# Turning the second image's columns back on ScalarE with accumulating transfers, residuals in the banks, and seven products one group earlier

## The chip, the cores and the metric

One core of a Trainium2 chip. The metric is the device time of one execution in microseconds (us), the median of several executions. The core's engines run side by side, each with a queue of its own: TensorE (PE in the profile) multiplies matrices out of SBUF, the on-chip memory of 128 partitions, into PSUM banks; VectorE (DVE) and ScalarE (ACT) work on SBUF and PSUM; GpSimd (POOL) does elementwise work and issues some transfers; SyncE (SP) only issues transfers. An instruction starts when the one ahead of it in its queue is done and what it waits for has come, so one late operand holds up everything behind it on that engine.

## The reference

The input is two images of 56 x 56 positions (tokens) with 384 channels in float32, 6272 tokens in all, and two layers. Cut to what matters here (LN is a layer norm over channels, gelu the exact one):

```
# layer 0: neighbourhood attention (7 x 7, 12 heads), then a two-layer product
x = x + attention(LN(x)) @ w_proj + b_proj
x = x + gelu(LN(x) @ w1 + b1) @ w2 + b2            # 384 -> 1536 -> 384
# layer 1: convolution and four directional scans, then a two-layer product
p     = LN(x) @ w_in + b_in                        # 384 -> 768
local = depthwise_conv_3x3(p)
mixed = 0.25 * (lr(local) + rl(local) + tb(local) + bt(local)) + local
x = x + LN(mixed) @ w_out + b_out                  # 768 -> 384
x = x + gelu(LN(x) @ w1' + b1') @ w2' + b2'
```

`lr`, `rl`, `tb` and `bt` are running averages y[i] = 0.6 y[i-1] + 0.4 x[i] along the rows, forwards and backwards, and along the columns, both ways. `mixed` of one image needs the whole image: the last row of a column scan depends on the first.

## The kernel before, in words

**Phases.** The attention comes first and takes the first 815 us or so; the change doesn't touch it. Then `passes` runs two passes over groups of four tiles of 128 tokens (512 tokens). The first pass (`groups`, one single tile and twelve fours) does the two-layer product of layer 0 for group g and, one group behind, the projection by w_in (`project_in`), which stores p by channels in DRAM (`p_d`). The second pass (`dgroups`, twelve fours and a single tile) does layer 1's part behind the scans: hidden products (12 x 3 matmuls of 128x512 by `hidden`, with a GELU on ScalarE for each of the 12), the projection by w_out of the next group (`project_out`, six matmuls for each tile), and the second product (`tokens`, 12 matmuls of 128x384 for each tile, 48 for a group). I call these three stages of a group its hidden stage, its projection and its second product.

**Seven products.** From group `switch` (4) on, the second pass does a group's two products in another form: matrices are split in two by two blocks, and seven block products with sums around them take the place of eight (`hidden_by_seven`, `tokens_by_seven`). It needs sums of the weights' blocks (`sums_of_w1`, five subtractions, and `sums_of_w2`, four), sums of the group's input (`sums_of_input`, four, whose tile is `xsums`), all on GpSimd, and room in SBUF that the convolution's buffers (the pool `conv`) hold until it has ended.

**The convolution beside.** The convolution and the scans are jobs that an object `Beside` deals out in steps between the products. `beside.go(worth, own)` adds to an allowance of VectorE time (times `rate`, less the stage's own VectorE work) and takes steps while there is allowance left; a step is what lies between two `yield`s, and the number yielded is its estimated cost. `beside.later(issue, n)` puts an instruction off by n steps, so that an engine's queue gets it when what it waits for is near. `beside.behind()` looks at the next job, starts its loads and returns it. `beside.until(name)` runs all that is left up to a job, at once.

A `Band` (a block of 128 channels, up to 28 rows of an image) loads p, multiplies the centre tap (ScalarE, `centre`, L1283), adds eight taps on VectorE (L1301), stores the result to `loc_d` and `mix_d` (SyncE, L1309), scans it along the rows in both directions (VectorE, `both_ways`), scales it (ScalarE, L1316), and adds it into `mix_d` by an accumulating transfer that GpSimd issues (`add_to_mix`, L1320). There is a `Columns` for each image and channel block, once the image's bands are done: it loads `loc_d` (two halves, L1337), turns rows into columns (`turn`: for each half of the columns four copies of 128x392, L1344, by GpSimd for the first half of a job that nothing turned ahead, else by ScalarE), and scans the two sets of columns in both directions in place; then it turns the result back while it adds it to `mix_d`: `mixed` is loaded from `mix_d`, VectorE adds the scaled lines to it (`scalar_tensor_tensor`, L1369, four for each channel block), and `mixed` is stored to `mix_d`.

**Order.** Within an engine the order is the order of the calls in the code; no scheduler moves instructions. So the steps of the convolution fall between the products where the allowance runs out. In the first pass `beside.go` is called after each product; image 1's bands come up from group to group, its columns must be done before the last group of the pass, and image 2's bands and columns run on into the second pass, up to the switch.

**The second pass's plain groups.** For each tile `tokens` fills a PSUM bank (two banks, in turns), VectorE adds the residual to it (`tensor_tensor`, L1922) and SyncE stores the tile to the output (L1923). In the last plain group, ahead of the first tile, `beside.until((1, NI - 1))` finishes the convolution, `cctx.close()` gives its room back, and the sums of weights are issued. The first pass has a different form here: there the residual is copied into the bank ahead (`seeded`, by ScalarE), the products are added to it, and ScalarE copies the sum out (L1855). The layer norm of mixed goes through the row sums that `measure` takes of the transposed input (L1405) and a factor that `project_out` applies (L1446).

Of the kernel before, what the change touches and what calls it, by code (L numbers as in the profile page):

```python
# [33 lines left out]
F32 = mybir.dt.float32  # L34
# [79 lines left out]
class Beside:  # L114
# [29 lines left out]
    def run(self):  # L144
        while True:
            self.idle = not self.jobs
            if self.idle:
                yield None
                continue
            if not self.jobs[0].loaded:  # L150
                self.jobs[0].load()
                yield 5.0
            job = self.jobs.pop(0)
            yield from job.steps()
            self.finished.add(job.name)
# [21 lines left out]
def block_kernel(ctx: ExitStack, tc: tile.TileContext, ins: dict, out: bass.AP):  # L177
# [914 lines left out]
    def passes(xs, xn, w1, w2, between=lambda ps: None):  # L1092
# [9 lines left out]
        switch = 4  # L1102
# [132 lines left out]
        def flat(t):  # L1235
            return t.rearrange("p a b -> p (a b)")
# [20 lines left out]
        class Band:  # L1257
# [21 lines left out]
            def centre(self):  # L1279
                if self.loc is None:  # L1280
                    self.loc = half("loc", "work", 3)
                    r = self.lo - self.top
                    nc.scalar.activation(  # L1283
                        flat(self.loc[:, : self.n]), flat(self.pt[:, r : r + self.n]), AF.Copy,
                        scale=self.tap(0, 0),
                    )

            def steps(self):
                beside.behind(Band)
                if self.loc is None:  # L1290
                    self.centre()
                    yield 2.5
# [15 lines left out]
                for to in (loc_d, mix_d):  # L1308
                    beside.later(lambda to=to: nc.sync.dma_start(  # L1309
                        out=to[self.b][self.m, :, at], in_=flat(loc)))  # L1310
                both = half("both", "out", 4)[:, : self.n]
                yield from both_ways(both, loc)
                behind = beside.behind()
                if isinstance(behind, Band):
                    behind.centre()
                beside.later(lambda: nc.scalar.mul(flat(both), flat(both), share), 8)  # L1316
# [5 lines left out]
        class Columns:  # L1322
# [27 lines left out]
            def steps(self):  # L1350
                if not self.lines:

                    self.turn(nc.gpsimd.tensor_copy)
                    yield 2.5
                mixed, behind = [], None
                for c in range(2):
                    t = self.lines[c]
                    for step, took in enumerate(both_ways(t, t)):
                        if c == 0 and step == 0:
                            self.turn(nc.scalar.copy)  # L1360
                            for h in range(2):
                                mixed.append(half("mixed", "out", 4))
                                nc.sync.dma_start(out=flat(mixed[h]), in_=self.rows(mix_d, h))
                        yield took
                    if c == 1:
                        behind = beside.behind()
                    for h in range(2):
                        to = mixed[h][:, :, c * HALF : (c + 1) * HALF]
                        nc.vector.scalar_tensor_tensor(  # L1369
                            to, t[:, :, h * HALF : (h + 1) * HALF].rearrange("p w h -> p h w"),  # L1370
                            share, to, ALU.mult, ALU.add,
                        )
                        yield us(HALF / 2, 2.0)
                    if c == 0:
                        beside.behind()
                if isinstance(behind, Columns):
                    behind.turn(nc.scalar.copy)
                for h in range(2):
                    beside.later(lambda h=h: nc.sync.dma_start(
                        out=self.rows(mix_d, h), in_=flat(mixed[h])))  # L1380
# [90 lines left out]
        def project_in(g, hT, between=lambda: None, at=1):  # L1471
# [15 lines left out]
            while bands and bands[0][0] * T1 + min(bands[0][2] + 1, H) * W <= t0 + groups[g][1] * P:  # L1487
                b, lo, hi = bands.pop(0)
                beside.jobs += [Band(b, m, lo, hi) for m in range(NI)]
                if hi == H:  # L1490
                    beside.jobs += [Columns(b, m) for m in range(NI)]
# [404 lines left out]
        beside.rate = 0.93  # L1896
        for g, (t0, n) in enumerate(dgroups[:switch]):
# [7 lines left out]
            if g == switch - 1:  # L1905

                beside.until((1, NI - 1))
                cctx.close()
                tp = pctx.enter_context(tc.tile_pool(name="tail", bufs=1, reuse_waits="tile"))
                three = wp.tile([P, NC, INNER], F32, name="w1_t", tag="w_in")  # L1910
                w1_sums = sums_of_w1(w1, three)
                w2_sums, steps = sums_of_w2(w2)
                for step in steps:
                    step()
            for k in range(n):
                if k == n - 1:
                    hT = channels(xn, dgroups[g + 1][1], *n2)
                ps = tokens(hid, w2, k)
                o = res[:, k, :]
                if k == 0:  # L1920
                    norm.shift(dgroups[g + 1][1])
                nc.vector.tensor_tensor(o, ps, o, ALU.add)  # L1922
                nc.sync.dma_start(out=yout[t0 + k * P : t0 + (k + 1) * P, :], in_=o)  # L1923
# [3 lines left out]
                beside.go(ROW, STATS)  # L1927
# [144 lines left out]
```

## Time and profile before

| | us |
|---|---|
| time, median of 3 | 2593.29 (2593.11 to 2597.07) |
| profiled execution, its own time | 2597.85 |
| span of the profiled execution | 2596.0 |
| its mean TensorE clock, of full speed | 0.994 |

Busy time of each engine by stretch, from windows on the profile (us):

| stretch | what runs | PE | DVE | ACT | POOL |
|---|---|---|---|---|---|
| 0 to 820 | attention | 804.7 | 590.1 | 438.0 | 183.3 |
| 820 to 1070 | first pass, ahead of the convolution | 248.6 | 182.4 | 102.6 | 33.1 |
| 1070 to 1540 | first pass with the convolution | 468.4 | 383.2 | 215.0 | 64.5 |
| 1540 to 2010 | rest of the first pass, plain groups of the second | 453.2 | 383.1 | 147.7 | 85.5 |
| 2010 to 2596 | groups by seven products | 581.9 | 422.4 | 173.6 | 198.9 |

How such a profile is read: a row of the timeline is a run of like instructions with its start, the time it took, the engine, the line of the code, the operation and its operands (out<-in). What stands in brackets behind it is how long the engine had been idle ahead of the row, and which instruction's end released it. An engine that is busy nearly all the time sets the span; idle time of the others matters only where the busy one waits for it.

### The profile page before, as it was taken

Reading aid. Unit: us, or ns where it says so; the run is one execution under the profiler, and the core shown is the slowest. Engines: PE = TensorE matmul, PEld = TensorE weight load, DVE = VectorE, ACT = ScalarE, POOL = GpSimd, SP = SyncE. Lnnn points to the kernel's source line nnn. Section 1 sums busy time; section 2 is a strip of 40 time slices with the busy share of each in tenths; the row PEclk is TensorE's granted clock in tenths of the full one; section 3 lists DMA queues with packets and bytes.
Section 4 is the critical chain, followed back from the end, with each engine's and each line's share of the span. In section 5 each row is a group of like instructions: output and inputs, shape, how many; then the busy total and the mean of one; then the engine's idle time right before and its main releaser. Section 6 shows DMA issues by size and latency. Waiting matters only on the chain. (4 is left out here: it accounts for less than half of the span.)

```text
span 2596.0 us, 41217 instructions
## 1 busy us (share of the span) xinstructions
PE 2556.8 (98%) x16342; PEld 1679.8 (65%) x16342; DVE 1961.2 (76%) x3660; ACT 1076.8 (41%) x1943; POOL 565.4 (22%) x593
## 2 busy tenths in 40 slices
PE   9999999999999999999999999999998999999999
PEld 5666666666788644555545555455554888888888
DVE  4888878887344389967799979878886778878871
ACT  5655555654443344433555333322332232333222
POOL 0111212121532011110211101111105233333332
PEclk9999999999999999999999999999999999999999
DMA  7423454225412356545665567855763233333210
GB/s 230 153 83 99 157 194 144 81 94 194 129 43 61 92 160 166 157 128 151 209 236 213 172 165 214 247 132 173 246 216 105 55 73 74 73 74 74 46 28 21
DMA packets 163931, 348.10 MB, mean 134 GB/s; under 512 B 12326, under 2 KB 114192, under 8 KB 161424
## 3 DMA queue, kind: packets, MB, share of 16 engines
q1 hardware_dynamic: 131568, 270.45, 30.1%
q0 software_dynamic: 27216, 48.17, 11.7%
q10 hardware_dynamic: 4944, 26.74, 3.0%
q8 instruction: 130, 2.13, 0.3%
q14 instruction: 73, 0.60, 0.1%
HBM read 181.55 MB, written 134.88 MB: 122 GB/s over the span
## 5 line engine op out<-in xcount | busy, mean ns | idle before, releaser
L1301 DVE SCALAR_TENSOR_TENSOR loc<-pt,taps,loc 128x495 f32<-128x495 f32 (+13 forms) x432 | 398.2, 922 | 118.5 <-ACT loc L1283 105.0
L1195 PE MATMUL mm<-hT,w 128*128 128x512 f32 x936 | 413.1, 596 | 6.1 <-ACT hT L272 5.3
L1195 PEld LDWEIGHTS mm<-hT,w 128*128 128x128 f32 x936 | 175.8, 191 | 216.2 <-issue 201.5
L571 ACT ACTIVATE pts<-pts 119x448 f32<-119x448 f32 (+5 forms) x396 | 210.8, 573 | 110.3 <-DVE pts L561 105.8
L561 DVE TENSOR_TENSOR pts<-sc,bias 119x448 f32<-119x448 f32 (+5 forms) x396 | 219.2, 616 | 45.9 <-PE sc L550 45.6
L1213 PE MATMUL y<-w,hid 128*128 128x384 f32 x696 | 231.4, 490 | 10.8 <-DVE xc L1922 10.8
L1213 PE MATMUL y_end<-w,hid 128*128 128x384 f32 x696 | 229.2, 486 | 0.0
L404 PE MATMUL ps<-hT,wqkv 128*128 128x448 f32 x504 | 204.8, 550 | 2.1 <-ACT vs L449 1.5
L1206 ACT ACTIVATE hid<-mm,chan 128x512 f32<-128x512 f32 x156 | 106.8, 687 | 232.3 <-PE mm L1195 232.3
L1213 PEld LDWEIGHTS y<-w,hid 128*128 128x128 f32 x696 | 132.4, 191 | 102.2 <-DVE xc L1922 11.4
L1213 PEld LDWEIGHTS y_end<-w,hid 128*128 128x128 f32 x696 | 131.8, 190 | 90.6
L1178 DVE STREAM_TRANSPOSE hT<-xn 32x96 f32<-32x96 f32 x592 | 159.6, 270 | 23.2 <-ACT xn L255 15.5
L1417 DVE STREAM_TRANSPOSE turned<-mx 32x192 f32<-32x192 f32 x464 | 171.2, 369 | 6.1
L1195 PE MATMUL mm<-hT,w_in 128*128 128x512 f32 x396 | 172.2, 593 | 1.3 <-ACT mx L1476 0.8
L404 PEld LDWEIGHTS ps<-hT,wqkv 128*128 128x128 f32 x504 | 91.3, 189 | 84.4 <-issue 74.2
L227 POOL TENSOR_TENSOR rs<-rs,mhalf 128x4 f32<-128x4 f32 (+4 forms) x55 | 60.0, 1091 | 372.1 <-DVE rs L224 362.3
L1195 PEld LDWEIGHTS mm<-hT,w_in 128*128 128x128 f32 x396 | 75.0, 190 | 96.0 <-issue 90.4
L1320 POOL DMA_DIRECT2D mix_d<-both x54 | 50.9, 942 | 365.5 <-ACT both L1316 324.3
L550 PEld LDWEIGHTS sc<-qT,kT 32*100 32x100 f32 (+3 forms) x3168 | 87.8, 169 | 46.6 <-DVE sum L580 7.6
L590 PE MATMUL o<-pts,vt 100*32 100x112 f32 (+3 forms) x3168 | 116.5, 264 | 0.5 <-ACT pts L571 0.5
L620 PE MATMUL ps<-wproj,og 128*128 128x384 f32 x294 | 107.1, 504 | 2.8 <-DVE og L533 2.1
L550 PE MATMUL sc<-qT,kT 32*100 32x112 f32 (+3 forms) x3168 | 106.5, 268 | 3.2 <-DVE pts L561 3.2
(187 smaller groups left out, 4514.0 us busy)
## 6 DMA issues: line engine op xcount, KB each, us to landing
loc<-loc_d SPq DMA_DIRECT2D x24, 784.0 KB
mixed<-mix_d SPq DMA_DIRECT2D x24, 784.0 KB
mix_d<-mixed SPq DMA_DIRECT2D x24, 784.0 KB
xa<-x_d SPq DMA_DIRECT2D x24, 768.0 KB
xa<-rows POOLq DMA_DIRECT2D x24, 768.0 KB, 7.8
bias<-in_bias_t ACTq DMA_DIRECT2D x13, 1344.0 KB
p_d<-mx SPq DMA_DIRECT2D x11, 1536.0 KB
mx<-mix_d SPq DMA_DIRECT2D x11, 1536.0 KB
```

Of the source, the lines that this page charges most:

```text
L404: nc.tensor.matmul(ps, lhsT=wqkv[:, c, m * P : (m + 1) * P], rhs=hT[:, c, half_of(n)], start=c == 0, stop=c == NC - 1,)
L550: nc.tensor.matmul(sc[i // 2][: w.keys, i % 2, q : q + TT], lhsT=kT[d, hg, w.keys_at + r * w.kc : w.keys_at + (r + w.rows) * w.kc], rhs=qT ...
L561: nc.vector.tensor_tensor(self.pts[:n, h : h + 2, lo:hi, :], sc[half][:n, :, at * TT : (at + hi - lo) * TT].rearrange("p h (c q) -> p h c ...
L571: nc.scalar.activation(t, t, AF.Exp)
L590: nc.tensor.matmul(o[i * HD : (i + 1) * HD, self.slot, :TT], lhsT=w.vt[:n, c, h * HD : (h + 1) * HD], rhs=self.pts[:n, i, c, :], start=c = ...
L620: nc.tensor.matmul(ps, lhsT=ogs[t // 7][:, c, at : at + P], rhs=wproj[:, c, :], start=c == 0, stop=c == NC - 1,)
L1178: nc.vector.transpose(hT[j : j + HD, :, k * P + i : k * P + i + HD], xn[i : i + HD, k, :].rearrange("p (c q) -> p c q", c=NC)[:, :, j : j ...
L1195: nc.tensor.matmul(ps[:, : n * P], lhsT=w[:, c, m * P : (m + 1) * P], rhs=hT[:, c, : n * P], start=c == 0, stop=c == NC - 1,)
L1206: nc.scalar.activation(t[:, : n * P], ps[:, : n * P], AF.Gelu, bias=col(b1, m))
L1213: nc.tensor.matmul(ps, lhsT=t[:, k * P : (k + 1) * P], rhs=w[:, m, :], start=m == 0 and onto is None, stop=m == len(lhs) - 1, skip_group_c ...
L1301: nc.vector.scalar_tensor_tensor(to, pt[:, lo + dy - self.top : hi + dy - self.top, xt : xt + n], self.tap(dy, dx), to, ALU.mult, ALU.add,)
L1417: nc.vector.transpose(t[j : j + HD].rearrange("p (m c) -> p m c", m=NI)[:, :, i : i + HD], mx[i : i + HD, :, k * P + j : k * P + j + HD],)
```

## The change

- `switch` is 3 instead of 4: one more group goes by seven products.
- Image 2's `Columns` no longer load `mix_d`. Their lines are scaled and turned back by ScalarE into `mixed` (`turn_back`: eight `mul` of 128x392 for each channel block), and two accumulating transfers on GpSimd's queue add it to `mix_d`. Image 1's keep the addition on VectorE.
- A plain group of the second pass copies the residual into the bank ahead (`seeded`), and ScalarE copies the sum out, in place of VectorE's addition. The end of the convolution and the sums of weights move from ahead of the group's first tile to ahead of its third (k == 2).
- Smaller moves: stores of a band come four steps later, a column's store three; the next job is looked at before a band's scans rather than behind them, and after the first scan of a set of columns; a band can have its next job's columns turned by ScalarE and a column its next job's centre tap made; a centre tap that nothing made ahead goes to VectorE; the yield behind a job's first load is 8.0 instead of 5.0; two columns that aren't loaded yet move behind newly listed bands; the second pass's rate of 0.93 is gone, and its second product no longer takes 0.75 us off each allowance.

```diff
@@ Beside.run
-                yield 5.0
+                yield 8.0
@@ passes
-        switch = 4
+        switch = 3
@@ Band
-            def centre(self):
+            def centre(self, engine=nc.scalar):
                 if self.loc is None:
...
-                    nc.scalar.activation(
-                        flat(self.loc[:, : self.n]), flat(self.pt[:, r : r + self.n]), AF.Copy,
-                        scale=self.tap(0, 0),
-                    )
+                    to, src = flat(self.loc[:, : self.n]), flat(self.pt[:, r : r + self.n])
+                    if engine is nc.scalar:
+                        nc.scalar.activation(to, src, AF.Copy, scale=self.tap(0, 0))
+                    else:
+                        nc.vector.tensor_scalar_mul(to, src, self.tap(0, 0))
 
             def steps(self):
                 beside.behind(Band)
                 if self.loc is None:
-                    self.centre()
-                    yield 2.5
+                    self.centre(nc.vector)
+                    yield us(self.n)
...
                 for to in (loc_d, mix_d):
                     beside.later(lambda to=to: nc.sync.dma_start(
-                        out=to[self.b][self.m, :, at], in_=flat(loc)))
+                        out=to[self.b][self.m, :, at], in_=flat(loc)), 4)
                 both = half("both", "out", 4)[:, : self.n]
+                behind = beside.behind()
                 yield from both_ways(both, loc)
-                behind = beside.behind()
                 if isinstance(behind, Band):
                     behind.centre()
+                if isinstance(behind, Columns):
+                    behind.turn(nc.scalar.copy)
@@ Columns.steps
+                def turn_back(c):
+                    if not mixed:
+                        mixed.extend(half("mixed", "out", 4) for h in range(2))
+                    for i in range(0, HALF, QUARTER):
+                        at = slice(c * HALF + i, c * HALF + i + QUARTER)
+                        for h in range(2):
+                            nc.scalar.mul(
+                                mixed[h][:, :, at],
+                                self.lines[c][:, i : i + QUARTER, h * HALF : (h + 1) * HALF]
+                                .rearrange("p w h -> p h w"), share,
+                            )
+
                 for c in range(2):
                     t = self.lines[c]
                     for step, took in enumerate(both_ways(t, t)):
                         if c == 0 and step == 0:
                             self.turn(nc.scalar.copy)
-                            for h in range(2):
+                            for h in range(2) if self.b == 0 else ():
                                 mixed.append(half("mixed", "out", 4))
                                 nc.sync.dma_start(out=flat(mixed[h]), in_=self.rows(mix_d, h))
                         yield took
-                    if c == 1:
-                        behind = beside.behind()
-                    for h in range(2):
-                        to = mixed[h][:, :, c * HALF : (c + 1) * HALF]
-                        nc.vector.scalar_tensor_tensor(
-                            to, t[:, :, h * HALF : (h + 1) * HALF].rearrange("p w h -> p h w"),
-                            share, to, ALU.mult, ALU.add,
-                        )
-                        yield us(HALF / 2, 2.0)
-                    if c == 0:
-                        beside.behind()
+                        if step == 0:
+                            behind = beside.behind()
+                    if self.b == 0:
+                        for h in range(2):
...
+                    else:
+                        beside.later(lambda c=c: turn_back(c), 1 + c)
                 if isinstance(behind, Columns):
                     behind.turn(nc.scalar.copy)
+                if isinstance(behind, Band):
+                    behind.centre()
                 for h in range(2):
-                    beside.later(lambda h=h: nc.sync.dma_start(
-                        out=self.rows(mix_d, h), in_=flat(mixed[h])))
+                    if self.b == 0:
+                        beside.later(lambda h=h: nc.sync.dma_start(
+                            out=self.rows(mix_d, h), in_=flat(mixed[h])), 3)
+                    else:
+                        at = slice(h * HALF * W, (h + 1) * HALF * W)
+                        beside.later(
+                            lambda h=h, at=at: add_to_mix(self.b, self.m, at, mixed[h]), 3
+                        )
@@ project_in
-                beside.jobs += [Band(b, m, lo, hi) for m in range(NI)]
+                last = [j for j in beside.jobs if isinstance(j, Columns) and not j.loaded][-2:]
+                beside.jobs = [j for j in beside.jobs if j not in last]
+                beside.jobs += [Band(b, m, lo, hi) for m in range(NI)] + last
@@ second pass, plain groups
-        beside.rate = 0.93
...
-            if g == switch - 1:
-
-                beside.until((1, NI - 1))
-                cctx.close()
...
+            seeds = [seeded(res, k) for k in range(2)]
             for k in range(n):
+                if g == switch - 1 and k == 2:
+
+                    beside.until((1, NI - 1))
+                    cctx.close()
...
-                ps = tokens(hid, w2, k)
-                o = res[:, k, :]
+                ps = tokens(hid, w2, k, onto=seeds.pop(0))
                 if k == 0:
                     norm.shift(dgroups[g + 1][1])
-                nc.vector.tensor_tensor(o, ps, o, ALU.add)
-                nc.sync.dma_start(out=yout[t0 + k * P : t0 + (k + 1) * P, :], in_=o)
                 if k == n - 3:
                     xn = normalized(norm, x3, dgroups[g + 1][1])
                     add_row(x3, dgroups[g + 1][1], "b2_1")
-                beside.go(ROW, STATS)
+                beside.go(ROW)
+                o = res[:, k, :]
+                nc.scalar.copy(o, ps)
+                nc.sync.dma_start(out=yout[t0 + k * P : t0 + (k + 1) * P, :], in_=o)
+                if k + 2 < n:
+                    seeds.append(seeded(res, k + 2))
```

## The prediction, made before the changed kernel ran

> **What bounds the kernel now.** I read the page's busy shares first, then TensorE's waits, then TensorE's timeline over the second half, and last the other engines' timelines around TensorE's two long gaps.
>
> ```profile
> PE 2556.8 (98%) x16342; PEld 1679.8 (65%) x16342; DVE 1961.2 (76%) x3660; ACT 1076.8 (41%) x1943; POOL 565.4 (22%) x593
> ```
>
> TensorE (PE) is the bound: 98% of a span of 2596.0 us. So the change can gain only by giving PE less work or by closing PE's gaps, and can lose only by opening gaps. Nearly all the idle time lies in these two waits (start, us, what; the gap ahead of the row is in brackets):
>
> ```profile
> 1553.01 10.46 PE L1195 MATMUL mm<-hT,w 128*128 128x512 f32 x24
> ...
> 1674.49 13.07 PE L1195 MATMUL mm<-hT,w 128*128 128x512 f32 x24 [5.30 <-ACT hT L272]
> ...
> 1758.38 10.46 PE L1195 MATMUL mm<-hT,w 128*128 128x512 f32 x24
> ...
> 1839.66 10.46 PE L1195 MATMUL mm<-hT,w 128*128 128x512 f32 x24
> ...
> 1969.95 7.90 PE L1213 MATMUL y<-w,hid 128*128 128x384 f32 x24
> ...
> 1996.39 9.99 PE L1213 MATMUL y<-w,hid 128*128 128x384 f32 x24 [10.79 <-DVE xc L1922]
> ...
> 2015.86 1.03 PE L1547 MATMUL ua<-hT,w 128*128 128x256 f32 x4
> ...
> 2087.59 1.03 PE L1547 MATMUL ua<-hT,w 128*128 128x256 f32 x4
> ```
>
> Two things are to be seen. A plain group of the second pass takes 1839.66 - 1758.38 = 81.28 us of PE, a group by seven products 2087.59 - 2015.86 = 71.73. And each gap costs more than itself: the same 24 matmuls take 13.07 instead of 10.46 behind one, 9.99 instead of 7.90 behind the other.
>
> What ended the gaps stands in ScalarE's (ACT) and GpSimd's (POOL) timelines:
>
> ```profile
> 1673.05 0.71 ACT L1283 ACTIVATE loc<-pt,taps 128x504 f32<-128x504 f32 x1 [4.45 <-DMA pt<-p_d]
> 1673.67 2.10 ACT L272 ACTIVATE hT<-tp,chan 128x512 f32<-128x512 f32 x3
> ```
> ```profile
> 1979.76 4.81 POOL L1515 TENSOR_TENSOR w_t<-w,w_t 128x768 f32<-128x768 f32 x1
> 1984.52 1.80 POOL L1515 TENSOR_TENSOR w_t<-w 128x768 f32<-128x768 f32 x1
> ...
> 2001.08 2.62 POOL L1605 TENSOR_TENSOR w_t<-w 128x1152 f32<-128x1152 f32 x1
> ```
>
> At 1673 the eviction that PE needs (hT) stands in ACT's queue behind a centre tap of a band, which waits for its transfer. At 1986 VectorE (DVE) is working off what is left of the convolution at the switch to seven products, and the residual add that frees a bank is queued behind it.
>
> **The skill beside the trace.** The Trainium skill, "TensorE: Matmul & The Clock Gate", Part 1, says that the array's clock is halved after an idle window of about 3.4 us and comes back after as long a busy one. The trace agrees in size: 2.61 and 2.09 us lost behind gaps of 5.30 and 10.79. I price a long gap at itself plus 2.1 to 2.6. "GPSIMD Engine Reference", section 1, says that POOL shares its SBUF interfaces with DVE and collides with DVE instructions of two SBUF inputs. The trace agrees: a scan of 128x1568 takes 4.98 us at 1977.98 against 3.42 elsewhere, and the POOL sum beside it 4.81 against 1.80. So the forecast takes POOL's sums at 1.80 and 2.62 where no scan runs beside them.
>
> **The change, part by part**, against the profiled execution's 2597.85 us (span 2596.0; the median of the runs is 2593.29, 4.56 lower).
>
> *Seven products from group 3.* One group of 81.28 becomes one of 71.73: -9.55. Nothing hides this, since PE is the bound.
>
> *The gap at 1669.* Stores to loc_d and mix_d now come four steps later, and the neighbours of bands start a step apart from before. In the built order the input load that was late (issued at 1660.98 behind the weight loads, landing at 1673.05) now feeds a centre tap that stands behind the three hT evictions and the first GELU of the group. With three banks of products PE can run three products (7.7 us) before it misses the next GELU: to about 1680. The load lands some 7 us earlier than that. The gap and the slow matmuls behind it go: -5.30 - 2.61 = -7.9. If the order shifts back, 0.
>
> *DVE's load up to the switch.* Removed: 24 additions of a turned-back half (6 channel blocks of image 2, four each), 1.58 us from start to start: -38 us. Also 12 residual adds of 0.55. What is left must end 81.28 us earlier. Counted from the built order with durations of the trace, DVE gets 28.7, 13.9 and 29.1 us in the three stages (hidden products, output projection, second product) of group 0, 26.8, 15.4 and 28.3 in group 1, 29.5 and 15.4 in group 2, beside 33.6, 15.5 and 32.3 us of PE. It keeps up, barely in the projection, where a scan of 3.4 us may stand ahead of an eviction; two banks forgive about 3.2 us.
>
> *ScalarE's load.* The additions become 8 scaled copies for each channel block, 48 in all. No row shows them; the nearest is the turning copy of the same size and stride (L1344, 128x392, 0.92 us, 0.855 from start to start). From below 0.52 (a dense scaling of 128x504 takes 0.62), from above 2 x 0.855 if the short output rows cost as much again; I take 0.855. The blocks follow each other through the second product of group 1, the hidden stage and the projection of group 2: ACT gets 35.1, 31.1 and 11.2 us there, against 32.3, 33.6 and 15.5 of PE. That is a full queue, where it had 11.2, 14.0 and at most 6.8. Followed in order: ACT ends the second product some 4 us late, the first GELU of group 2 goes at once, the next one waits for eight turning copies (6.8 us), and PE misses its bank by about 1.3 us. The banks seeded at the end of the projection stand behind eight turning copies as well, with 0.7 us to spare. Together I charge +3.0 (0 to 8).
>
> *Transfers.* The image-2 loads and stores of mix_d (24 of 784 KB, SP's queue) become 12 accumulating writes on POOL's queue. The nearest row, 504 KB, lands in 7.1 us and costs POOL 0.94. Behind a write that waits for ACT stand norm powers and row additions, needed a stage later: 0. Loads of loc take 7 us (1799.89 to 1806.78) and have 11.
>
> *The gap at the switch.* It goes in its old form: evictions by ACT no longer wait for DVE, and only a scan is left. What is late next is POOL. In its queue the weight sums now stand behind the last two accumulating writes, and the sums of the input, which the seven products need at once, behind all nine weight sums. From the start T of group 2's second product: DVE ends the last block's projections, norm and two scans at T+14.5; ACT's four copies at 17.9; POOL issues two writes to 19.9; five sums of 1.80 and four of 2.62 end at 39.4; the first input sum at 40.1. PE comes there at T+33.9 (the stage takes 33.0 without its stall, then 0.86). Gap 6.2 and 2.1 of slow clock: 8.3 in place of 10.79 + 2.09 = 12.9, so -4.6. If the sums take 25.5 us, as before beside DVE's scans, the gap is 12.4 and nothing is gained; if the convolution ends early, all of 12.9 is.
>
> *Small things.* A centre tap by DVE where none was made ahead, longer allowances, the rate 1.0: in the DVE count above. Seeds: two copies of 0.48 for each tile, in ACT's count.
>
> Sum: -9.55 - 7.9 - 4.6 + 3.0 = -19.05. Profiled 2578.8; against the median **2574.2 us**.
>
> **Rivals.**
> 1. *Half of it.* Product saving kept, but either the gap at 1669 stays, or POOL's sums are slow or late. 9.55 + 4.6 - 3.0 = 11.2 (2582) for the first; 9.55 + 7.9 - 3.0 = 14.5 (2579) for the second; both, with the gap at the switch 2 us longer: 4.5 (2589). For it: POOL's serial queue. Against: the order of ACT's queue.
> 2. *ScalarE becomes the bound (slower).* Place: group 1's second product to group 2's projection, where ACT has 4.0 us to spare over 81.4. There are 32 scaled copies there; each 0.1 us above 0.855 costs 3.2 us. Above 0.98 the spare is gone, at 1.75 the loss (28.7 - 4) eats the gain and 5 more; at 2.0 the time is 2574 + 32.6 = 2606. Against: the read is the turning copy's.
> 3. *No stall anywhere at the switch.* The sums overlap the tail of the second product: 2574.2 - 8.3 = 2566.
> 4. *DVE falls behind in the projections*: up to 3 us at each of three stages and the flush as much later: about 10 us, 2584; with rival 1, no change.
>
> **How the numbers follow.** 0.2% (5.2 us) is what a measurement of this kernel tells from no change. Likeliest case 0.42 (its own range 2568 to 2580), rivals 1 and 4 0.33, of them 0.05 within 0.2%, rival 3 0.05, no change by other mixtures 0.08, rival 2 and other losses 0.12. Faster 0.42 + 0.28 + 0.05 = 0.75; same 0.13; slower 0.12. The range leaves out rival 2's losses and the far end of rival 3: 2565 to 2592.
>
> **What would show it.** Plain groups of the second pass fall from four to three and 71.7 us groups rise from eight to nine. No gap near 1669. Scaled copies near 0.9 us. At the switch a gap of 6 us ahead of the first product with xsums, ended by POOL. In group 2's hidden stage a gap of 1 to 3 us ended by a GELU. Wrong would be: scaled copies above 1.2 us, gaps ended by ACT in every projection, or POOL's sums again at 3 to 5 us.

## The result, and the profile after

The changed kernel takes 2603.58 us (median of 15 runs, 2598.37 to 2608.2), the kernel before 2597.07 (15 runs beside them). The ratio is 1.0026 with an interval of 1.0017 to 1.0036: slower by a quarter of a per cent, where 2574.2 us was forecast (against 2593.29 for the kernel before). The span of the profiled execution is 2603.0 us against 2596.0.

The page's busy shares of the kernel after:

```profile
PE 2554.5 (98%) x16438; PEld 1697.8 (65%) x16438; DVE 1957.9 (75%) x3763; ACT 1137.1 (44%) x2043; POOL 569.3 (22%) x619
```

PE is as busy as before, although a group has gone over to fewer products. So work was saved, and slow matmuls and gaps have taken its place. TensorE's waits of the kernel after, the longest first (us in total, times, longest):

```profile
PE mm L1195 <- ACT mx L1501: 6.8, 2, 6.0
PE mm L1195 <- ACT hid L1206: 6.4, 4, 3.6
PE uz L1574 <- POOL xsums L1555: 5.5, 1, 5.5
PE y_end L1213 <- ACT y_end L1223: 3.7, 1, 3.7
```

Both waits of before (10.8 on VectorE at the switch, 5.3 on hT) are gone. In their place there are four, three of them on ScalarE. TensorE's timeline of the kernel after shows where they are (the rows count each float32 product of the code twice, so that the 12 of a tile are x24 here):

```profile
1285.47 4.60 PE L1195 MATMUL mm<-hT,w_in 128*128 128x512 f32 x6 [5.96 <-ACT mx L1501]
...
1515.10 2.84 PE L1195 MATMUL mm<-hT,w 128*128 128x512 f32 x6 [1.69 <-ACT hid L1206]
1519.54 15.72 PE L1195 MATMUL mm<-hT,w_in 128*128 128x512 f32 x36 [1.60 <-ACT hT L272]
...
1684.92 10.57 PE L1195 MATMUL mm<-hT,w 128*128 128x512 f32 x24 [0.65 <-ACT hT L272]
...
1844.72 9.70 PE L1213 MATMUL y_end<-w,hid 128*128 128x384 f32 x24 [3.74 <-ACT y_end L1223]
...
1863.04 2.84 PE L1195 MATMUL mm<-hT,w 128*128 128x512 f32 x6 [0.89 <-ACT hid L1206]
...
1870.14 8.38 PE L1195 MATMUL mm<-hT,w 128*128 128x512 f32 x12 [3.61 <-ACT hid L1206]
...
1950.68 2.07 PE L1574 MATMUL uz<-xsums,w_t 128*128 128x256 f32 x4 [5.53 <-POOL xsums L1555]
```

The gap near 1669 is 0.65 us now (the row at 1684.92). Two gaps stand in the first pass (1285, and the pair near 1517), where none was forecast; three around 1840 to 1870, in group 1's second product and group 2's hidden stage; one at the switch.

From the starts of the stages in the two timelines (a stage's time is the next one's start less its own) the 7.0 us between the spans come out as follows:

| stage | before | after | difference |
|---|---|---|---|
| up to the first plain first-pass group (attention above all) | 905.8 | 908.9 | +3.1 |
| first-pass projection at 1263 / 1267 | 16.76 | 24.74 | +8.0 |
| first-pass hidden stage at 1473 / 1484 | 32.21 | 35.93 | +3.7 |
| last w_in projection at 1652 / 1667 and the hidden stage behind it | 58.47 | 51.56 | -6.9 |
| group 1's projection and second product, group 2's hidden stage | 81.28 | 95.69 | +14.4 |
| last plain second product and the hidden stage behind it, by seven products | 71.41 | 65.64 | -5.8 |
| a plain group less, a group by seven products more | 81.28 | 71.4 | -9.9 |
| the rest | | | +0.4 |

The first row is no effect of the change: in the profiles of this study that stage starts anywhere between 901.6 and 911.1 us, with the same code ahead of it. For the same reason spans of single profiles that lie less than 9 us apart are not compared below; stages and medians are, and, where it is said, the time of a profile from that stage's start to its end. The runs below were taken in three sets, with the kernel before measured anew beside each: its medians lie between 2598.54 and 2600.58 us (2597.07 in the result above), so a difference of 2 to 4 us between medians of different sets shows nothing. The ratios are to the kernel before of the same set.

Why ScalarE was late at 1840 stands in its own timeline of the kernel after:

```profile
1827.62 4.19 ACT L1366 ACTIVATE mixed<-line 128x392 f32<-128x392 f32 x5
1841.27 2.52 ACT L1366 ACTIVATE mixed<-line 128x392 f32<-128x392 f32 x3 [9.47 <-DMA mix_d<-mixed]
1843.70 0.46 ACT L1953 COPY xc<-y_end 128x384 f32<-128x384 f32 x1
1844.19 0.48 ACT L1223 COPY y_end<-xc 128x384 f32<-128x384 f32 x1
1844.61 6.67 ACT L1347 COPY line<-loc 128x392 f32<-128x392 f32 x8
1851.18 0.71 ACT L1319 ACTIVATE both<-both 128x616 f32<-128x616 f32 x1
```

Of the 8 scaled copies of the second channel block, one starts and the next waits 9.47 us for an accumulating write to land, with the eviction and the seed of a bank (L1953, L1223) behind it. The copies themselves take what was forecast (five in 4.19 us; 0.855 each was forecast). The write that ends the wait is the first block's, issued at 1830.47. The buffer it frees comes from the four that `both` and `mixed` share (`half(..., "out", 4)`). At that moment the first block holds two, the second block's first half one, and the fourth is held by the last band's `both`: its scaling, put off by eight steps, comes only at 1851.18, behind the wait and 54 us after the end of its scan (1797.4). In the kernel before the same scaling came 13.7 us after its scan (1803.3 and 1817.05): there a channel block of image 2 took eight steps, four scans and four additions, and with the additions gone it takes four, so that eight steps now reach over two blocks.

At 1285 ScalarE's timeline of the kernel after shows this:

```profile
1272.42 0.91 ACT L1347 COPY line<-loc 128x392 f32<-128x392 f32 x1
1279.06 5.78 ACT L1347 COPY line<-loc 128x392 f32<-128x392 f32 x7 [5.73 <-DMA loc<-loc_d]
1284.75 1.83 ACT L1501 ACTIVATE mx<-mm,chan 128x512 f32<-128x512 f32 x3
```

Eight turning copies stand ahead of the projection's evictions (L1501), and the second of them waits 5.73 us for the second half of the lines to land. Four of the eight are new there: a band now has the next job's columns turned by ScalarE, where GpSimd turned them before. At the same place of the kernel before, ScalarE has four copies, and a wait of 2.65 us among them that TensorE doesn't feel:

```profile
1271.89 0.92 ACT L1344 COPY line<-loc 128x392 f32<-128x392 f32 x1
1275.45 2.58 ACT L1344 COPY line<-loc 128x392 f32<-128x392 f32 x3 [2.65 <-DMA loc<-loc_d]
1277.94 1.81 ACT L1476 ACTIVATE mx<-mm,chan 128x512 f32<-128x512 f32 x3
```

### The profile page after: what moved, and what is told of

The parts are those of the page before. It is cut to its first block, busy times and chain, and to the rows that moved or that the text cites. A ratio compares the mean times of both kernels' runs of the same rounds, so it can differ in the third digit from the quotient of the medians.

```text
span 2603.0 us, 41611 instructions
## 1 busy us (share of the span) xinstructions
PE 2554.5 (98%) x16438; PEld 1697.8 (65%) x16438; DVE 1957.9 (75%) x3763; ACT 1137.1 (44%) x2043; POOL 569.3 (22%) x619
## 3 DMA queue, kind: packets, MB, share of 16 engines
q1 hardware_dynamic: 128064, 251.18, 28.5%
## 5 line engine op out<-in xcount | busy, mean ns | idle before, releaser
L1195 PE MATMUL mm<-hT,w 128*128 128x512 f32 x864 | 382.3, 597 | 7.0 <-ACT hid L1206 6.4
L1195 PEld LDWEIGHTS mm<-hT,w 128*128 128x128 f32 x864 | 162.5, 191 | 203.2 <-issue 185.6
L1213 PE MATMUL y_end<-w,hid 128*128 128x384 f32 x648 | 215.2, 489 | 3.7 <-ACT y_end L1223 3.7
L1213 PE MATMUL y<-w,hid 128*128 128x384 f32 x648 | 213.6, 486 | 0.5 <-ACT y L1223 0.5
L1442 DVE STREAM_TRANSPOSE turned<-mx 32x192 f32<-32x192 f32 x528 | 194.9, 369 | 20.6 <-DMA mix_d<-mixed 13.7
L1178 DVE STREAM_TRANSPOSE hT<-xn 32x96 f32<-32x96 f32 x656 | 176.8, 269 | 26.0 <-ACT xn L255 17.5
L1213 PEld LDWEIGHTS y_end<-w,hid 128*128 128x128 f32 x648 | 123.5, 191 | 89.4 <-ACT y_end L1223 4.0
L1213 PEld LDWEIGHTS y<-w,hid 128*128 128x128 f32 x648 | 122.3, 190 | 84.5 <-ACT y L1223 1.1
L1206 ACT ACTIVATE hid<-mm,chan 128x512 f32<-128x512 f32 x144 | 98.5, 688 | 180.3 <-PE mm L1195 180.3
L1248 DVE TENSOR_TENSOR_SCAN line<-decay,line 128x1568 f32<-128x1568 f32 x24 | 81.9, 3414 | 41.3 <-ACT line L1347 41.3
```

Of the source, the lines that this page charges most:

```text
L1178: nc.vector.transpose(hT[j : j + HD, :, k * P + i : k * P + i + HD], xn[i : i + HD, k, :].rearrange("p (c q) -> p c q", c=NC)[:, :, j : j ...
L1195: nc.tensor.matmul(ps[:, : n * P], lhsT=w[:, c, m * P : (m + 1) * P], rhs=hT[:, c, : n * P], start=c == 0, stop=c == NC - 1,)
L1206: nc.scalar.activation(t[:, : n * P], ps[:, : n * P], AF.Gelu, bias=col(b1, m))
L1213: nc.tensor.matmul(ps, lhsT=t[:, k * P : (k + 1) * P], rhs=w[:, m, :], start=m == 0 and onto is None, stop=m == len(lhs) - 1, skip_group_c ...
L1442: nc.vector.transpose(t[j : j + HD].rearrange("p (m c) -> p m c", m=NI)[:, :, i : i + HD], mx[i : i + HD, :, k * P + j : k * P + j + HD],)
```

## The experiments

Theory A: three separate waits cost what the change had gained, each by the place of an instruction in a queue or of a buffer in its ring. Rival theory: ScalarE simply has too much to do (and VectorE the room that the change spared it), so that mending one wait brings up the next. The first edits are made on the changed kernel.

**No turning by ScalarE at a band's end.**

```diff
                 if isinstance(behind, Band):
                     behind.centre()
-                if isinstance(behind, Columns):
-                    behind.turn(nc.scalar.copy)
```

> Leaves out only the two new lines with which a band has the next job's columns turned by ScalarE; GpSimd turns that half again. Theory A (these four copies, and the wait for their transfer, stand ahead of the projection's evictions in ScalarE's queue): the TensorE gap of 5.96 us ahead of 1285 and the two of 1.69 and 1.60 near 1517 go or fall below 1, time 9 to 11 us below the changed kernel, ratio to the kernel before about 0.999. Rival B (the later stores and earlier looks at the next job make the load late whoever turns): the gap stays above 3 us, behind the other four copies, and the time falls by less than 4 us.

Measured: 2595.5 us (ratio to before 0.9985, 0.9978 to 0.9993), 8.1 below the changed kernel, somewhat short of the 9 to 11 expected. The projection at 1265 takes 16.76 us again instead of 24.74, the hidden stage at 1474 takes 32.88 instead of 35.93. That is 11.0 us in the first pass. The whole is less, since about 2 us come back in the hidden stage at 1555 (36.87 against 34.84) and the wait at the switch is 2.4 longer (7.9 against 5.5). ScalarE's wait for a buffer near 1840 is still there, and TensorE now stands still behind it once, for 9.0 us.

**The last band's buffer freed early.**

```diff
-                beside.later(lambda: nc.scalar.mul(flat(both), flat(both), share), 8)
-                beside.later(lambda: add_to_mix(self.b, self.m, at, both), 11)
+                soon = isinstance(behind, Columns) and behind.b == 1
+                beside.later(lambda: nc.scalar.mul(flat(both), flat(both), share), 1 if soon else 8)
+                beside.later(lambda: add_to_mix(self.b, self.m, at, both), 2 if soon else 11)
```

> Scales and adds the row scan of the last bands of image 2 one and two steps behind its end instead of eight and eleven, so that its buffer is free before the second channel block is turned back. Theory A (the wait for a buffer makes ScalarE late): no ScalarE wait of 9.5 us near 1832, the second product of group 1 and the hidden stage of group 2 fall from 38.1 and 41.5 us to about 33.5 and 36, time 8 to 13 us below the changed kernel. Rival B (ScalarE has simply too much to do there): the wait is replaced by others, the two stages lose less than 4 us together.

Measured: 2590.61 us (0.997, 0.996 to 0.9979), 13.0 below the changed kernel. ScalarE's timeline at the same place, with no wait:

```profile
1825.25 6.65 ACT L1367 ACTIVATE mixed<-line 128x392 f32<-128x392 f32 x8
1831.81 0.45 ACT L1954 COPY xc<-y_end 128x384 f32<-128x384 f32 x1
1832.30 0.48 ACT L1223 COPY y_end<-xc 128x384 f32<-128x384 f32 x1
1832.71 6.71 ACT L1348 COPY line<-loc 128x392 f32<-128x392 f32 x8
```

And the busy times by stage of this run (the second product of group 1, then the hidden stage and the projection of group 2; columns: window, its length, then PE, PEld, DVE, ACT and POOL busy with their instructions, TensorE's clock, DMA share, GB/s):

```profile
1813.80:1846.20 32.40, 32.38 (x109) 19.62 (x110) 28.92 (x18) 31.34 (x43) 5.69 (x7) 1.00 0.88 228
1846.20:1879.70 33.50, 33.50 (x97) 16.11 (x96) 28.59 (x24) 29.03 (x39) 3.37 (x4) 1.00 0.87 211
1879.70:1895.20 15.50, 15.50 (x49) 9.12 (x48) 13.86 (x15) 14.18 (x18) 5.78 (x3) 1.00 1.01 275
```

ScalarE is busy 74.55 of 81.4 us, scaled copies included, and PE has no gap in these stages but the 0.45 us ahead of the first. With the projection ahead of them they take 81.99 us, where the kernel before took 81.28 and the changed one 95.69. So the rival theory falls for this place: one buffer cost 13.7 us, and the amount of ScalarE's work at most 0.7.

**The sums of the input ahead of w2's sums.**

```diff
@@ group switch - 1, k == 2
                     w2_sums, steps = sums_of_w2(w2)
-                    for step in steps:
-                        step()
@@ behind the loop
         xsums = sums_of_input(hT)
+        for step in steps:
+            step()
```

> Moves the four sums of w2's blocks behind the four sums of the input in GpSimd's queue; nothing else. Theory A (GpSimd's serial queue is what TensorE waits for at the switch): the gap of 5.53 us ahead of the product with xsums and the slow matmuls behind it go, the hidden stage of the first group by seven products falls from 33.2 to about 26 us, time 6 to 7.5 us below the changed kernel. Rival B (the input itself is late, or sums of weights collide with VectorE beside): the gap stays above 2 us.

Measured: 2596.12 us (0.9989, 0.998 to 0.9998), 7.5 below the changed kernel. The first hidden stage by seven products takes 25.43 us instead of 33.20, and no gap is left ahead of it. GpSimd's timelines, the changed kernel first and then this run:

```profile
1937.72 1.81 POOL L1542 TENSOR_TENSOR w_other<-w 128x768 f32<-128x768 f32 x1
1939.48 2.62 POOL L1632 TENSOR_TENSOR w_t<-w 128x1152 f32<-128x1152 f32 x1
...
1947.33 2.62 POOL L1632 TENSOR_TENSOR w_t<-w,w_t 128x1152 f32<-128x1152 f32 x1
1949.90 0.73 POOL L1555 TENSOR_TENSOR xsums<-hT 128x256 f32<-128x256 f32 x1
```
```profile
1937.20 1.81 POOL L1542 TENSOR_TENSOR w_other<-w 128x768 f32<-128x768 f32 x1
1938.96 0.73 POOL L1555 TENSOR_TENSOR xsums<-hT 128x256 f32<-128x256 f32 x1
1939.77 0.72 POOL L1555 TENSOR_TENSOR xsums<-xsums,hT 128x256 f32<-128x256 f32 x1
```

The input's first sum stood 10.4 us behind sums that TensorE first uses 50 us later (the product of w_t and s at 1999.73).

**The three together.**

> The three edits together. If their causes are separate, as theory A has them, the gains add up: 23 to 31 us below the changed kernel, ratio to the kernel before 0.988 to 0.994, about 2574 us. If one wait only hides behind another, the sum is less than 15 us.

Measured: 2574.93 us (0.9904, 0.9886 to 0.9922), 28.65 below the changed kernel; the three alone add up to 28.5. That the two agree so well is luck. Counted in the profiles from the first plain first-pass group to the end, the three alone save 7.4, 12.5 and 7.6 us, 27.5 in all, and the three together 22.3. So each of the three waits has a cause of its own, which its own edit takes away, but about 5 us come back in new waits when all three are gone: so far the rival theory is right.

**Mended once more.** In the three together the first-pass hidden stage at 1551 took 38.80 us instead of 34.84, with a wait of 2.08 us for the load of the mixed image 1 and slow matmuls behind it. Group 2's hidden stage still took 36.76 us and the first one by seven products 28.74: GpSimd now turned image 2's first columns too (at 1786), and the end of the convolution came late: VectorE, idle for 20.14 us until the mixed image was there, began with the transposes of that image 4.3 us into that hidden stage (1925.10 against 1920.8), and the sums that TensorE needs stood behind them. So GpSimd turns image 1's columns, ScalarE image 2's:

```diff
-                    behind.turn(nc.scalar.copy)
+                    behind.turn(nc.gpsimd.tensor_copy if behind.b == 0 else nc.scalar.copy)
```

> The early slot and the input sums ahead of w2's sums as before; the columns of image 1 are turned ahead by GpSimd at the band's end instead of by ScalarE, those of image 2 by ScalarE as in the change. Theory A (what is left in the three edits together is the loss of ScalarE's early turning for image 2, which makes the mixed image late at the switch): hidden stage of group 2 back from 36.8 to 33.5 us, first group by seven products from 28.7 to about 25.5, time 2564 to 2569 us, ratio to the kernel before about 0.988. Rival B: a gap of a few us comes back in the first pass or at the switch, and the time stays within 2572 to 2578.

Measured: 2573.63 us (0.9911, 0.9892 to 0.993), so that rival B has the total. The two stages are at 33.53 and 25.44 as expected, the one at 1551 (here 1558) is back at 34.84, and the transposes begin 0.4 us ahead of the hidden stage. The first-pass projection, though, rose from 16.76 to 20.94 us: ScalarE's other four copies wait 5.20 us there for the second half, since a job whose first half is turned ahead reaches them one eviction earlier than in the first run, where they waited 2.73. From the first plain group on, the profile is 6.7 us shorter than that of the three together, while the medians, from different sets, differ by 1.3: why they don't fall as far stays open. The next runs undo one part of the change at a time on this mended kernel.

**Seven products from group 4 on** (`switch = 4` in the mended kernel).

> The mended kernel with seven products from group 4 on, all else the same. Theory A (a group by seven products is worth 9.85 us, and the convolution keeps up with either switch): 9 to 11 us above the mended kernel. Rival B (the earlier switch crowds the convolution and gives back part of its gain): less than 6 us above it.

Measured: 2584.83 us (0.9954, 0.994 to 0.9969), 11.2 above the mended kernel. The earlier switch is worth its 9.9 us, and no stage gives any of it back.

**Image 2's additions by VectorE, as before** (the condition `self.b == 0` left out at its three places, so that both images take that path).

> The mended kernel with image 2's columns added by VectorE to a loaded mix, as image 1's, seven products from group 3 on. VectorE has 24 additions of 1.58 us more and some 18 us of room up to the switch, so the convolution ends about 20 us later. Theory A (the moved additions are what makes room for the earlier switch): a gap of 8 to 15 us at the switch, time 12 to 20 us above the mended kernel, no better than the kernel before by more than 0.7%. Rival B (VectorE had the room): less than 4 us above the mended kernel.

Measured: 2604.47 us (1.0025, 1.0016 to 1.0034), 30.8 above the mended kernel, more than expected. TensorE's longest wait in this run, and GpSimd's timeline:

```profile
PE uz L1575 <- POOL xsums L1556: 26.8, 1, 26.8
```
```profile
1902.34 1.80 POOL L1543 TENSOR_TENSOR w_t<-w 128x768 f32<-128x768 f32 x1
1938.12 3.09 POOL L1543 TENSOR_TENSOR w_t<-w,w_t 128x768 f32<-128x768 f32 x1 [33.98 <-DVE line L1252]
```

The fourth sum of w1 needs room that the convolution holds, and waits 33.98 us for VectorE's last scan. VectorE has 38 us more to do (24 times 1.58), and TensorE waits for 27 of them. So the move of the additions to ScalarE and the transfers is what makes the earlier switch pay.

**Residuals by VectorE, as before** (no seeds, `tensor_tensor` from the bank in place of ScalarE's copy).

> The mended kernel with the residual of plain second-pass groups added by VectorE from the bank, no seeds, as in the kernel before. Theory A (an eviction behind scans in VectorE's queue stops TensorE only where more than two scans stand ahead, at the end of the convolution): a gap of 2 to 6 us in the second product of group 2, time 2 to 8 us above the mended kernel. Rival B (VectorE's queue is short enough by then): within 1 us of the mended kernel.

Measured: 2572.2 us (0.9912, 0.9892 to 0.9931): the same as the mended kernel, as rival B has it. In the mended kernel that part of the change is worth nothing. (The later place of the end of the convolution, ahead of the third tile, is kept in this run; it was not tested alone, nor were the small moves, except for a band's stores and the turning at its end.)

**GpSimd turns both halves of image 1's first columns.**

```diff
                         if c == 0 and step == 0:
-                            self.turn(nc.scalar.copy)
+                            self.turn(nc.gpsimd.tensor_copy if self.by_pool else nc.scalar.copy)
```

`by_pool` is set where a band has turned them by GpSimd.

> The mended kernel, and for the first column job of image 1 behind a band GpSimd turns the second half as well, so that ScalarE turns neither. Theory A (what is left of the first-pass gap is ScalarE's wait for the transfer of the second half of the lines, with the projection's evictions behind it): the gap of 2.2 us near 1280 goes and that projection falls from 20.9 to 16.8 us, time 3 to 5 us below the mended kernel, about 2569. Rival B (VectorE or GpSimd is late for it and something behind waits): within 2 us of the mended kernel.

Measured: 2572.37 us (0.9891, 0.9876 to 0.9906), 1.3 below the mended kernel, which was in another set; by the ratios it would be some 5 us. The projection is back at 16.76 us, as theory A has it, but the hidden stage at 1558 takes 36.46 instead of 34.84, with a wait of 1.43 us on the load of the mixed image 1. So 1.6 of the 4.2 us are given back there. The total, four runs whose interval overlaps the mended kernel's, decides for neither theory.

**The kernel before with the stores four steps later.**

```diff
-                        out=to[self.b][self.m, :, at], in_=flat(loc)))
+                        out=to[self.b][self.m, :, at], in_=flat(loc)), 4)
```

> The kernel before with only one edit: a band's two stores come four steps later. Theory A (the order of the band's transfers removed the gap at 1669): the wait of 5.3 us goes, 7 to 8 us below the kernel before. Rival B (the gap went because the jobs themselves stand elsewhere in the first pass, or through the earlier look at the next job): the gap stays at 4 to 6 us and the time is the kernel before's within 2 us.

Measured: 2591.41 us (0.9969, 0.9955 to 0.9982), 9.2 below the kernel before beside it. The gap at 1669 falls from 5.30 to 0.74 us, and the projection with the hidden stage behind it from 58.47 to 51.40. SyncE's timelines, of before and of this run:

```profile
1660.12 0.34 SPq L1309 DMA_DIRECT2D loc_d<-loc  x1
1660.51 0.43 SPq L1309 DMA_DIRECT2D mix_d<-loc  x1
1660.98 0.43 SPq L1270 DMA_DIRECT2D pt<-p_d  x1
```
```profile
1662.19 0.34 SPq L1270 DMA_DIRECT2D pt<-p_d  x1
1662.58 0.43 SPq L1309 DMA_DIRECT2D loc_d<-loc  x1
1663.05 0.43 SPq L1309 DMA_DIRECT2D mix_d<-loc  x1
```

Issued ahead of the two stores, the load has landed when its centre tap runs at 1670.56, at most 8.4 us later; issued behind them it took 12.07 us, from 1660.98 to 1673.05. The weight loads stand ahead of it in both.

**The kernel before with seven products from group 3 on** (`switch = 3`, nothing else).

> The kernel before with only one edit: seven products from group 3 on. Theory A (without the moved additions VectorE cannot end the convolution a group earlier): what is left is worked off at the switch, a gap of 30 to 55 us there in place of 10.8, time 10 to 35 us above the kernel before. Rival B (the convolution has the room): 5 to 10 us below it.

Measured: 2641.09 us (1.016, 1.0146 to 1.0174), 40.5 above the kernel before beside it. TensorE's longest wait:

```profile
PE y L1213 <- DVE xc L1922: 62.8, 1, 62.8
```

It is 62.8 us where 10.8 was, more than the 30 to 55 expected. The saved group doesn't come near paying for it. (This run lacks all of the change but the switch, so it doesn't say by itself which part is missing; the run with VectorE's additions does.)

## Why the prediction was wrong, step by step

**Seven products: right.** Forecast -9.55, measured -9.9 by stages, and 11.2 by switching it back.

**The gap at 1669: right, in size and in its reason.** Forecast -7.9, measured -6.9. In ScalarE's queue of the changed kernel the centre tap stands where the forecast put it, behind the three hT evictions and the first GELU:

```profile
1684.10 2.11 ACT L272 ACTIVATE hT<-tp,chan 128x512 f32<-128x512 f32 x3
1687.80 0.69 ACT L1206 ACTIVATE hid<-mm,chan 128x512 f32<-128x512 f32 x1 [1.59 <-PE mm L1195]
1692.78 0.72 ACT L1285 ACTIVATE loc<-pt,taps 128x504 f32<-128x504 f32 x1 [4.29 <-DMA pt<-p_d]
```

The tap waits for its load nearly as long as before (4.29 and 4.45 us), and TensorE doesn't notice. What the forecast had too good is the load, which was to land some 7 us earlier than needed. In the kernel before with the stores alone moved, the gap goes in another way: there the tap still runs ahead of the hT evictions (1670.56 and 1671.16), and its load lands in time because it is issued ahead of the stores.

**DVE's load up to the switch: right.** The last scan ends 14.5 us after the start of group 2's second product, as forecast, and the two runs with the additions left on VectorE show what else would have happened (27 and 63 us of wait at the switch).

**The switch: right.** Forecast a gap of 6.2 us ahead of the product with xsums and -4.6 in all; measured 5.53 and -5.8. GpSimd's sums, all but the first (2.30), took 1.81 and 2.62 us, the figures taken for sums with no scan beside them. Where a scan of VectorE did run beside them, one was slow again: 4.82 us for one of w1's in the mended kernel with VectorE's additions, about the 4.81 of the kernel before. It fits what the Trainium skill says in "GPSIMD Engine Reference", section 1, that the two engines share their SBUF interfaces and collide where a VectorE instruction has two SBUF inputs; the section gives no size for it.

**ScalarE's load: wrong, the term of 14.4 us.** Forecast +3.0 (0 to 8) from counting ScalarE's work by stage. The price of a copy was right (0.83 us from start to start), and so was the queue's fill (77.4 us forecast for the three stages, 74.55 in the second run). The step that failed is the one under *Transfers* that put the accumulating writes at 0: it looked at what stands behind them in GpSimd's queue, and not at who waits for the buffers they read. The ring has four buffers, a channel block takes two, and the last band's `both` keeps a third for eight steps that now reach over two blocks. The chance of rival 2 (ScalarE as the bound, slower) was put on this place, but its mechanism was not the one: at 0.83 us for a copy it would have cost at most 0.7 us, as the second run shows.

**Left out of the sum: 11.7 us in the first pass.** The new lines with which a band has the next columns turned by ScalarE were not costed in any part. They were lumped with the small moves, whose cost was looked for in VectorE's count alone and only up to the switch. The run without them has 11.0 of the 11.7 us back. It isn't the four copies alone: with GpSimd making them at the band's end, as in the mended kernel, 4.2 of the projection's 8.0 us stay, because the lines also bring ScalarE's other four forward, to where their load has not landed. Each new instruction on ScalarE ahead of an eviction had to be followed to the transfer that it waits for, in the first pass too.

Sum by these terms: the forecast of -19.05, + 11.4 for ScalarE, + 11.7 for the first pass, and -0.6 for the rest of the terms gives +3.5, the stages' +3.9 without the attention to within 0.4. With the three waits taken out the time is 2574.93 us. That it meets the forecast of 2574.2 is luck: the forecast kept 3.0 us for ScalarE and 8.3 at the switch, which are mended in that run, and the kernel before beside it was 5 us slower than the one the forecast started from. The terms of gain alone, with nothing left at the switch, make 30.4 us (9.55, 7.9 and 12.9). The mended kernel has 25.4 of them and the last version 28.2, each against the kernel before beside it. So the gain was there, and the waits ate it.

## What to carry to other kernels

When work moves to another engine, its busy time is the smaller question: ScalarE was busy for 92% of three stages at a cost of 0.7 us at most, while one wait in its queue cost 13.7. So follow each moved instruction to the buffer that it writes, list who holds the ring's other buffers at that moment and which late instruction frees them; a delay counted in steps grows when other work leaves the steps. And read every added line once for each pass that runs it, not only for the stage that it was made for.

## What was not expected of the hardware

A TensorE gap of about the same length was followed by slow matmuls in three runs and by none in a fourth. It stands at the same place of the first pass. The mended kernel, after 2.22 us, and the same with VectorE's additions, after 2.37 us, in this order:

```profile
1279.81 4.54 PE L1195 MATMUL mm<-hT,w_in 128*128 128x512 f32 x6 [2.22 <-ACT mx L1502]
```
```profile
1276.66 2.84 PE L1195 MATMUL mm<-hT,w_in 128*128 128x512 f32 x6 [2.37 <-ACT mx L1502]
```

The granted clock in 3 us behind the gap (from 1280 and from 1277) was 0.51 in the first and 1.00 in the second. The mended kernel with switch 4 (2.33 us) and the one with VectorE's residuals (2.12 us) go with the first: the granted clock behind the gap is 0.67 in both, and the six matmuls take 4.34 and 4.30 us. The Trainium skill ("TensorE: Matmul & The Clock Gate", Part 1) gives the window as about 3.4 us, running freely, and has the clock halved after an idle one. Gaps of 2.12 to 2.33 us are shorter than that and were followed by a reduced clock. That the place of the gap in the window decides is a reading that would fit; no run here tests it.
